# Moving layer 2's products into the tail of layer 1, and layer 3's weight in front of its aggregation

## The chip, the cores and the metric

The kernel runs on one core of one Trainium2 chip. The metric is the device time of one execution in microseconds; the times given are medians over runs. All times inside an execution are counted from the start of its profiled span.

## The reference

Four graph layers on x (4096 x 256, float32) with one dense adjacency matrix `adj` (4096 x 4096, zeros and ones, with self loops). Every layer ends with x = layernorm(x + layer(x)).

```python
# layer 0: relu([x, (adj @ x) / max(deg, 1)] @ W + b)
# layer 1: two steps n = 0, 1 of
#   A  = top-p softmax attention of Xa (rows cut to mass 0.9, renormalised)
#   Xf = R @ Xf          (R: row-normalised adj + I)
#   Xa = A @ Xa
#   Z += Xf @ U1[n].T + Xa @ U2[n].T        then layernorm(X + Z) * g + b
# layer 2: [x, adj @ x, e] @ weight + bias  (e: one number per node)
# layer 3: relu((A_norm @ x) @ W + b),  A_norm = (adj + I) scaled by d^-1/2 on both sides
```

Layers 2 and 3 are linear before their bias, and in both the weight can be applied before the aggregation as well as after it: (adj @ x) @ W = adj @ (x @ W). The change rests on this.

## The kernel before

Rows are cut into 32 tiles of 128 (NT = 32, P = 128, D = 256). A product with the adjacency takes, for each output tile, 32 matmuls 128x512: the right side holds the upper and the lower half of each number side by side (`split`, L140: 2 x 256 columns in the type fp32r), the left side is the adjacency, brought from memory in four pieces of 512 KB per tile by POOL's DMA queue into four buffers (`adj_piece`, L135; `adj_matmul`, L162). The two 256-column halves of the result are added afterwards.

Layer 1 works through its tiles with attention. Rows whose cut cannot be settled in the common way are put off: they are listed, and gathered into put-off tiles (`put_off`, L836; four of them in step 1). A put-off tile is a generator with stages: rows and logits; then `peak` and the exponentials; five probes in `bracket` (L440), each a pass of VectorE over 4096 columns (L464); candidates, `tops`, `pick`, and `flag` (L548). The flag of a put-off tile is a matmul with a column of ones (L554) into the bank `mm_bank`, a copy by ScalarE (L556), and a read of the value by VectorE, which in `settle` (L607) branches on it at L614; `settle` then writes the kept weights over the tile `e`. `finish` (L903) draws the remaining stages of a put-off tile and then makes its sums in `pieces` (L691): transposes of `e` (L712) and matmuls with xa (L737). What follows a tile's sums is returned by `after` (L806): s1 is `mix` (L784: transposes, four matmuls with U1 and U2 at L790), s2 the two layernorms and the store of x2 (`put`, L755, an indirect store on POOL's queue for put-off tiles). These are passed on in a list `last` and placed among the next tile's `pieces`.

At the end of step 1 two put-off tiles are left in `jobs` (L988); the list `last` of the third is worked off within the sums of the fourth.

Then come layers 2 and 3 in one block (L1026). Layer 2 loads x2 as halves (`load_halves`, L147, eight loads of 512 KB through two scratch buffers). For each tile `main` (L1038) makes the 32 matmuls, and `l2_end` (L1043) adds the halves, loads the tile's own x2, transposes both (four transposes), multiplies with the 512 rows of the weight (four matmuls at L1052), adds bias and the edge term, normalises, stores x3, scales it by d^-1/2 and splits it into the halves `yh` that layer 3 aggregates. In layer 3 `l3_end` (L1065) adds halves, its own term (x3 scaled by `dinv2`), transposes (two), multiplies with w3 (two matmuls at L1075), adds bias, relu, the residual, and normalises. `main` of a tile stands ahead of the end of the tile before it:

```python
for halves, end in ((lambda jt: x2h[:, jt, :], l2_end), ...):
    for it in range(NT):
        new = main(it, halves)
        if acc is not None:
            end(it - 1, acc)
```

Each engine has its own queue of instructions, in an order fixed when the program is built; an engine whose next instruction waits holds up all that stand behind it. `mm_bank` is one PSUM bank of 512 float32 columns, used as two halves of 256 in turn (`half`, L78).

Of the kernel before, what the change touches and what calls it, by code (L numbers as in the profile page):

```python
# [21 lines left out]
P = 128  # L22
D = 256
# [25 lines left out]
def gnn_stack(ctx, tc, x, adjt, adjn, w0, b0, w1, w2t, w3t, u1t, u2t, ln_g, ln_b, w2, b2, w3, b3, out):  # L49
# [55 lines left out]
    x1b_d = dram.tile([N, D], F32, name="x1b_d")  # L105
    x2_d = dram.tile([N + P, D], F32, name="x2_d")
    x3_d = dram.tile([N, D], F32, name="x3_d")
    xa_d = dram.tile([N + P, D], F32, name="xa_d")
    xf_d = dram.tile([N, D], F32, name="xf_d")
    list_d = [dram.tile([N + P, 1], I32, name=f"list{n}_d") for n in range(STEPS)]  # L110
# [36 lines left out]
    def load_halves(scratch, src, queue):  # L147


        xh = hpool.tile([P, NT, 2 * D], F32R, tag="H", name="xh")  # L150
        W = J0 * D
        for c in range(NT // J0):
            s = slice(c * J0, (c + 1) * J0)
            t, up = (scratch[:, k * W : (k + 1) * W].rearrange("p (j d) -> p j d", d=D) for k in (c % 2, 2 + c % 2))
            if queue is None:
                t = src[:, s, :]
            else:
                queue.dma_start(t, all_rows(src)[:, s, :])
            split(up.bitcast(I32), xh[:, s, :], t)
        return xh  # L160

# [33 lines left out]
    def ln_apply(dst, t, stats):  # L195
        mv, r = stats
        nc.vector.tensor_scalar(dst, t, mv[:, 0:1], r, op0=ALU.subtract, op1=ALU.mult)
# [17 lines left out]
    with tc.tile_pool(name="l0", bufs=1) as l0, tc.tile_pool(name="l0w", bufs=2) as l0w:  # L215
# [68 lines left out]
        def l0_end(it, agg):  # L284
            xi = l0w.tile([P, D], F32, tag="x0i", name="x0i")
            nc.scalar.dma_start(xi, rows(x, it))
            xt = transposed(xi, agg)
            ps = half("mm")
            for c in range(4):
                nc.tensor.matmul(ps, xt[:, c, :], w0_sb[:, c, :], start=(c == 0), stop=(c == 3))  # L290
            t = l0w.tile([P, D], F32, tag="t", name="t")
            nc.vector.tensor_add(t, ps, b0_sb)
            nc.vector.scalar_tensor_tensor(t, t, 0.0, xi, op0=ALU.max, op1=ALU.add)
            ln_apply(x1[:, it, :], t, ln_stats(t))

# [3 lines left out]
            nc.sync.dma_start(rows(x1b_d, it), x1b)  # L299

        def l0_keys(it):
            make_keys(transposed(x1[:, it, :]), kS[:, it * P : (it + 1) * P])
# [18 lines left out]
    with tc.tile_pool(name="l1", bufs=1, reuse_waits="tile") as l1:  # L321
# [484 lines left out]
        def after(n, st):  # L806


            def s1():
                st["h"] = mix(n, st)  # L810

            def s2():
                h = st["h"]
                mv, r = ln_stats(h)
                nc.vector.scalar_tensor_tensor(h, h, mv[:, 0:1], cur["g"], op0=ALU.subtract, op1=ALU.mult)
                nc.vector.scalar_tensor_tensor(h, h, r, st["x1"], op0=ALU.mult, op1=ALU.add)
                ln_apply(h, h, ln_stats(h))
                put(x2_d, st, h)

            return [s1] if n + 1 < STEPS else [s1, s2]  # L820

        def take_rows(n, slots, e):

# [59 lines left out]
        def run_step(n, es):  # L883
# [16 lines left out]
                    job["st"] = st  # L900
                return False

            def finish(job, last):  # L903
                while not advance(job):
                    pass
                ops = {}
                for k, fs in enumerate(last):
                    ops[k + 1] = fs
                cur["late"] = True
                pieces(n, job["st"], None, ops)  # L910
                cur["late"] = False
                return [[f] for f in after(n, job["st"])]
# [64 lines left out]
            if n == 0:  # L977
# [46 lines left out]


    with tc.tile_pool(name="l23", bufs=1, reuse_waits="tile") as l23:  # L1026
        w2_sb = load_w(l23, w2[: 2 * D, :], "w2_sb")
# [4 lines left out]
        x2h = load_halves(l23.tile([P, 4 * J0 * D], F32, name="scratch"), x2_d[:N, :], nc.sync)  # L1032

        yh = [pool.tile([P, NT // 2, 2 * D], F32R, tag="X", name=f"yh{k}") for k, pool in enumerate((xpool, l23))]
        dinv2 = l23.tile([P, NT], F32, name="dinv2")
        nc.vector.tensor_mul(dinv2, dinv, dinv)

        def main(it, halves):  # L1038
            acc = ps_acc.tile([P, 512], F32, tag=("acc", "nef")[it % 2], name="acc")
            adj_matmul(l23, acc, it, halves, JP)  # L1040
            return acc

        def l2_end(it, acc):  # L1043
            nn = l23.tile([P, D], F32, tag="agg", name="agg", bufs=2)
            nc.scalar.copy(nn, acc[:, :D])
            nc.vector.tensor_add(nn, nn, acc[:, D:])
            xi = l23.tile([P, D], F32, tag="res", name="x2i", bufs=2)
            nc.sync.dma_start(xi, rows(x2_d, it))
# [6 lines left out]
            nc.vector.scalar_tensor_tensor(t, w2e_sb, nef[:, it : it + 1], ps, op0=ALU.mult, op1=ALU.add)  # L1055
            nc.vector.tensor_add(t, t, xi)
            x3 = l23.tile([P, D], F32, tag="h", name="x3", bufs=2)
            ln_apply(x3, t, ln_stats(t))
            nc.sync.dma_start(rows(x3_d, it), x3)
            y = l23.tile([P, 1, D], F32, tag="y", name="y", bufs=2)  # L1060
            nc.vector.tensor_scalar(y[:, 0, :], x3, dinv[:, it : it + 1], None, op0=ALU.mult)
            up = l23.tile([P, 1, D], I32, tag="up", name="up", bufs=2)
            split(up, yh[2 * it // NT][:, it % (NT // 2), None, :], y)

        def l3_end(it, acc):  # L1065
            x3 = l23.tile([P, D], F32, tag="res", name="x3i", bufs=2)
            nc.sync.dma_start(x3, rows(x3_d, it))
            a = l23.tile([P, D], F32, tag="agg", name="agg", bufs=2)
            nc.scalar.activation(a, acc[:, :D], AF.Copy, scale=dinv[:, it : it + 1])
# [6 lines left out]
            t = l23.tile([P, D], F32, tag="t", name="t", bufs=2)  # L1076
            nc.vector.tensor_add(t, ps, b3_sb)
            nc.vector.scalar_tensor_tensor(t, t, 0.0, x3, op0=ALU.max, op1=ALU.add)
            o = l23.tile([P, D], F32, tag="h", name="o", bufs=2)
            ln_apply(o, t, ln_stats(t))  # L1080
            nc.sync.dma_start(rows(out, it), o)

        for halves, end in ((lambda jt: x2h[:, jt, :], l2_end), (lambda jt: yh[2 * jt // NT][:, jt % (NT // 2), :], l3_end)):
            acc = None
            for it in range(NT):
                new = main(it, halves)
                if acc is not None:
                    end(it - 1, acc)
                acc = new
            end(NT - 1, acc)  # L1090


# [39 lines left out]
```

## Time and profile before

| | us |
|---|---|
| time, median of 3 | 3500.99 (3497.21 to 3509.62) |
| span of the profiled execution | 3453.8 |
| TensorE matmul busy | 3070.8 (89%) |
| VectorE busy | 2372.2 (69%) |
| ScalarE busy | 1596.2 (46%) |
| GpSimd busy | 962.0 (28%) |
| L168, matmuls of layer 0 and 2 (2048) | 547.7 |
| L168, matmuls of layer 3 (1024) | 257.5 |

The profile is of one execution, shorter than the timed ones; differences are read within it. Layer 0 fills the first 460 us or so, layer 1 ends at about 2826 us with its last store of x2, layer 2's matmuls run to about 3151 and layer 3's to 3438. Matmuls are recorded as pipelined, each with its end, so that their durations overlap, and an f32 matmul shows as two records, an fp32r matmul as one. DMA share is the mean busy share of the 16 DMA engines.

### The profile page before, as it was taken

To read this page: it belongs to the slowest core of one execution; us is meant where nothing else is said; L and a number is where in the kernel's file an instruction comes from. 1 tells how busy PE (TensorE), PEld (TensorE's weight loads), DVE (VectorE), ACT (ScalarE), POOL (GpSimd) and SP (SyncE) were. 2 spreads that over 40 slices of the span, in tenths; PEclk is the share of its full clock that TensorE was granted. 3 is DMA by queue.
4 is the path that set the end of the run, shared out by engine and by line. 5 is a ranking of instruction groups with operands and counts; after the bars stand their busy time and mean duration, and the time that the engine had idled before them with its cause. 6 is when DMAs were issued, how large, how long until landed. Compare 5 with 4: busy or idle time off the path is not lost. (4 is left out here: it accounts for less than half of the span.)

```text
span 3453.8 us, 46253 instructions
## 1 busy us (share of the span) xinstructions
PE 3070.8 (89%) x14780; PEld 2501.1 (72%) x14780; DVE 2372.2 (69%) x7082; ACT 1596.2 (46%) x2846; POOL 962.0 (28%) x1234
## 2 busy tenths in 40 slices
PE   6888878999999999779998898999998549999998
PEld 4666657788888887557787777877787437887776
DVE  5666676788778887447888897889799654443333
ACT  3443356677777776436555454555554211111000
POOL 1222224666666666200000001000100112222332
PEclk8999989999999999789999999999999769999999
DMA  6777756777777776431000211011010038888886
GB/s 215 228 224 213 218 127 105 133 138 138 137 133 134 138 147 133 115 111 42 24 24 22 34 33 35 26 36 35 28 38 22 15 98 246 244 245 245 266 266 214
DMA packets 252192, 433.86 MB, mean 126 GB/s; under 512 B 35136, under 2 KB 177280, under 8 KB 251936
## 3 DMA queue, kind: packets, MB, share of 16 engines
q0 software_dynamic: 92544, 289.11, 34.8%
q1 hardware_dynamic: 142416, 125.73, 13.0%
q10 hardware_dynamic: 16976, 15.95, 1.5%
q8 instruction: 119, 1.95, 0.3%
q14 instruction: 137, 1.12, 0.1%
HBM read 423.45 MB, written 57.54 MB: 139 GB/s over the span
## 5 line engine op out<-in xcount | busy, mean ns | idle before, releaser
L652 PE MATMUL acc_r<-xh,adjq 128*128 128x512 f32 x2048 | 615.4, 431 | 22.8 <-ACT adjq L649 17.6
L168 PE MATMUL acc<-xh,adjt 128*128 128x512 f32 x2048 | 547.7, 422 | 92.3 <-DMA adjt<-in_adjt 65.5
L737 PE MATMUL acc_bank<-xa,at 128*128 128x256 f32 x2304 | 563.3, 385 | 30.1 <-ACT at L715 29.6
L638 POOL DMA_INDIRECT G<-x_d,cols x512 | 502.0, 981 | 281.9 <-PE acc_bank L729 153.3
L168 PEld LDWEIGHTS acc<-xh,adjt 128*128 128x128 f32 x2048 | 400.3, 200 | 204.5 <-DMA adjt<-in_adjt 74.1
L737 PEld LDWEIGHTS acc_bank<-xa,at 128*128 128x128 f32 x2304 | 421.7, 192 | 90.7 <-ACT at L715 40.7
L652 PEld LDWEIGHTS acc_r<-xh,adjq 128*128 128x128 f32 x2048 | 380.7, 192 | 118.2 <-ACT adjq L649 42.9
L649 ACT CAST adjq<-adj 128x512 fp32r<-128x512 uint8 x512 | 316.0, 619 | 292.9 <-PE acc_r L652 94.5
L399 DVE MAX8 cand<-e 128x8 f32<-128x256 f32 x1024 | 381.5, 415 | 92.0 <-ACT e L381 91.0
L137 POOL DMA_DIRECT2D adjt<-in_adjt x384 | 209.4, 545 | 700.3 <-PE acc L168 346.9
L380 PE MATMUL lg<-kS,q 128*128 128x512 f32 x1104 | 393.4, 442 | 9.8 <-ACT e L381 9.6
L381 ACT COPY e<-lg 128x512 f32<-128x512 f32 x552 | 319.5, 585 | 177.6 <-PE lg L380 176.5
L192 POOL TENSOR_TENSOR rstd<-ve,mhalf 128x1 f32<-128x1 f32 x168 | 107.7, 641 | 843.8 <-DVE ve L190 797.5
L729 PE MATMUL acc_bank<-G,dg 128*128 128x256 f32 x1024 | 274.7, 389 | 39.8 <-DMA G<-x_d,cols 24.9
L496 DVE FIND_INDEX8 cols<-top,e 128x8 uint32<-128x4096 f32 x64 | 282.8, 4419 | 0.0
L168 PE MATMUL acc<-yh,adjt 128*128 128x512 f32 x1024 | 257.5, 403 | 4.7 <-DMA adjt<-in_adjt 4.4
L729 PEld LDWEIGHTS acc_bank<-G,dg 128*128 128x128 f32 x1024 | 194.3, 193 | 87.5 <-DMA G<-x_d,cols 36.1
L715 ACT COPY at<-at_ps 128x512 f32<-128x512 f32 x296 | 173.7, 589 | 145.3 <-PE at_ps L712 143.9
L168 PEld LDWEIGHTS acc<-yh,adjt 128*128 128x128 f32 x1024 | 190.0, 188 | 50.3 <-PE tr L178 4.5
L712 PE MATMUL at_ps<-ident,e 128*128 128x128 f32 x1184 | 183.8, 279 | 39.8 <-DVE e L629 26.9
L712 PEld LDWEIGHTS at_ps<-ident,e 128*128 128x128 f32 x1184 | 152.0, 145 | 75.6 <-issue 34.2
L380 PEld LDWEIGHTS lg<-kS,q 128*128 128x128 f32 x1104 | 183.5, 193 | 31.8 <-ACT e L381 18.5
(274 smaller groups left out, 4583.3 us busy)
## 6 DMA issues: line engine op xcount, KB each, us to landing
adjt<-in_adjt POOLq DMA_DIRECT2D x384, 512.0 KB
adj<-adj_d SPq DMA_DIRECT2D x256, 128.0 KB
adj_d<-a SPq DMA_DIRECT2D x128, 128.0 KB
adjn<-in_adjn POOLq DMA_DIRECT2D x64, 256.0 KB
x_d<-x SPq DMA_DIRECT2D x64, 128.0 KB
G<-x_d,cols POOLq DMA_INDIRECT x512
xf_d<-xf_new SPq DMA_DIRECT2D x64, 128.0 KB
xf<-xf_d SPq DMA_DIRECT2D x64, 128.0 KB
```

The costliest lines, as they stand in the source:

```text
L137: nc.gpsimd.dma_start(t, src[it, :, c * jp : (c + 1) * jp, :])
L168: nc.tensor.matmul(acc, a[:, j, :], halves(jt), start=(jt == 0), stop=(jt == NT - 1))
L380: nc.tensor.matmul(pl[:, :LC], q[k], kS[:, s], start=(k == 0), stop=(k == 1))
L381: nc.scalar.copy(l[:, s], pl[:, :LC])
L399: nc.vector.max(dst[:, 8 * g : 8 * g + 8], src[:, g * GW : (g + 1) * GW])
L496: nc.vector.max_index(st["at"][:, 8 * r : 8 * r + 8], t8, st["e"][:, :N])
L638: nc.gpsimd.indirect_dma_start(out=g, out_offset=None, in_=x1_d, in_offset=bass.IndirectOffsetOnAxis(ap=st["at"][:, k : k + 1], axis=0))
L649: nc.scalar.copy(a, cur["a8"][:, g % 2 * GP : (g % 2 + 1) * GP, :])
L652: nc.tensor.matmul(acc_r, a[:, j, :], xf[:, jt, :], start=(jt == 0), stop=False)
L712: nc.tensor.transpose(ps[:, j, :], e[:, (g * G + j) * P : (g * G + j + 1) * P], ident)
L729: nc.tensor.matmul(acc_a, dg[:, k % 4, :], st["G"][k], start=(k == 0), stop=(k == KEPT - 1))
L737: nc.tensor.matmul(acc_a, ats[g][:, j, :], cur["xa"][:, jt, :], start=(jt == 0), stop=(jt == NT - 1))
```

## The change

Three parts belong together.

1. x2 is multiplied with layer 2's weight already in layer 1. A new tensor zu in memory holds for each row 512 numbers: z = x2 @ (rows of the weight that belong to the neighbours), and u = x2 @ (rows that belong to the node itself). Before the last put-off tile of step 1 is finished, `last` is worked off, the weight is loaded into a tile `e` that is free by then (`z_room`), and after each stage of the put-off tile that `finish` draws, three of the 32 tiles of zu are made (`zu_tile`): load the tile of x2, two transposes, two f32 matmuls of 128x512, a copy by ScalarE, a store. Since `zu` needs 512 columns it writes the whole of `mm_bank`. The rows of the last put-off tile get their zu after their x2 is known.
2. Layer 2 aggregates the halves of z, so that after the aggregation no product is left: `l2_end` adds the halves, the edge term, u, x2 and the bias. It loads one more tile (u) than before.
3. Layer 3's weight is applied to layer 2's result, before the aggregation (`l2_y`, two tiles later in the order): two transposes and two matmuls, then ScalarE scales by d^-1/2 and the result is split. `l3_end` has no product left; it takes its own term from `yh`.

Part 1's order in TensorE's queue, as the changed program has it: the flag's matmul of the last put-off tile stands behind the transposes of 30 zu tiles and the matmuls of 27.

The diff, cut to its core:

```diff
+        def z_room(e):
+            w = e[:, : 4 * D].rearrange("p (c o) -> p c o", c=2)
+            for k in range(2):
+                nc.sync.dma_start(w[:, :, k * D : (k + 1) * D],
+                                  w2[(1 - k) * D : (2 - k) * D, :].rearrange("(c p) o -> p c o", p=P))
+            cur["z"] = {"w": w, "x": e[:, 4 * D : 8 * D].rearrange("p (k o) -> p k o", o=D),
+                        "out": e[:, 8 * D : 16 * D].rearrange("p (k o) -> p k o", o=2 * D), "n": 0}
+        def zu(x):
+            z = cur["z"]
+            xt = transposed(x)
+            ps = mm_bank.rearrange("p h o -> p (h o)")
+            for c in range(2):
+                nc.tensor.matmul(ps, xt[:, c, :], z["w"][:, c, :], start=(c == 0), stop=(c == 1))
+            out = z["out"][:, z["n"] % 4, :]
+            z["n"] += 1
+            nc.scalar.copy(out, ps)
+            return out
+        def zu_tile(i):
+            x = cur["z"]["x"][:, i % 4, :]
+            nc.sync.dma_start(x, rows(x2_d, i))
+            nc.sync.dma_start(rows(zu_d, i), zu(x))
...
-            def finish(job, last):
+            def finish(job, last, todo=()):
                 while not advance(job):
-                    pass
+                    for i in todo[:3]:
+                        zu_tile(i)
+                    todo = todo[3:]
+                for i in todo:
+                    zu_tile(i)
...
-            for job in jobs:
-                last = finish(job, last)
+            for k, job in enumerate(jobs):
+                todo = []
+                if n > 0 and k + 1 == len(jobs):
+                    for fs in last:
+                        for f in fs:
+                            f()
+                    last = []
+                    z_room(es[1 - NT % 2])
+                    todo = list(range(NT))
+                last = finish(job, last, todo)
...
         def l2_end(it, acc):
...
-            xt = transposed(xi, nn)
-            ps = half("mm")
-            for c in range(4):
-                nc.tensor.matmul(ps, xt[:, c, :], w2_sb[:, c, :], start=(c == 0), stop=(c == 3))
+            u = l23.tile([P, D], F32, tag="u", name="u", bufs=2)
+            nc.sync.dma_start(u, rows(zu_d, it)[:, D:])
             nc.vector.tensor_add(xi, xi, b2_sb)
+            nc.vector.tensor_add(u, u, xi)
...
+        def l2_y(it, x3):
+            xt = transposed(x3)
+            ps = half("mm")
+            for c in range(2):
+                nc.tensor.matmul(ps, xt[:, c, :], w3_sb[:, c, :], start=(c == 0), stop=(c == 1))
             y = l23.tile([P, 1, D], F32, tag="y", name="y", bufs=2)
-            nc.vector.tensor_scalar(y[:, 0, :], x3, dinv[:, it : it + 1], None, op0=ALU.mult)
+            nc.scalar.activation(y[:, 0, :], ps, AF.Copy, scale=dinv[:, it : it + 1])
...
         def l3_end(it, acc):
...
-            nc.vector.scalar_tensor_tensor(a, acc[:, D:], dinv[:, it : it + 1], a, op0=ALU.mult, op1=ALU.add)
-            nc.vector.scalar_tensor_tensor(a, x3, dinv2[:, it : it + 1], a, op0=ALU.mult, op1=ALU.add)
-            xt = transposed(a)
-            ps = half("mm")
-            for c in range(2):
-                nc.tensor.matmul(ps, xt[:, c, :], w3_sb[:, c, :], start=(c == 0), stop=(c == 1))
+            own = y_halves(it).bitcast(F32)
+            for part in (own[:, :D], own[:, D:], acc[:, D:]):
+                nc.vector.scalar_tensor_tensor(a, part, d, a, op0=ALU.mult, op1=ALU.add)
```

More of the change, by code (lines that the diff above doesn't have):

```diff
@@ L107, in gnn_stack @@
     x3_d = dram.tile([N, D], F32, name="x3_d")
+    zu_d = dram.tile([N + P, 2 * D], F32, name="zu_d")
     xa_d = dram.tile([N + P, D], F32, name="xa_d")
@@ L145, in split, with load_halves @@
         nc.vector.tensor_sub(dst[:, :, D:], src, up.bitcast(F32))
-    def load_halves(scratch, src, queue):
+    def load_halves(scratch, src, queue, cols=slice(None)):
         xh = hpool.tile([P, NT, 2 * D], F32R, tag="H", name="xh")
@@ L157, in load_halves @@
             else:
-                queue.dma_start(t, all_rows(src)[:, s, :])
+                queue.dma_start(t, all_rows(src)[:, s, cols])
             split(up.bitcast(I32), xh[:, s, :], t)
@@ L299, in l0_end @@
             nc.sync.dma_start(rows(x1b_d, it), x1b)
+            if it == NT - 1:
+                nc.sync.dma_start(rows(x2_d, it), x1[:, it, :])
         def l0_keys(it):
@@ L818, in s2 @@
                 put(x2_d, st, h)
+                if "z" in cur:
+                    put(zu_d, st, zu(h))
             return [s1] if n + 1 < STEPS else [s1, s2]
+        def z_room(e):
[19 more added lines that the diff above has]
+            nc.sync.dma_start(rows(zu_d, i), zu(x))
         def take_rows(n, slots, e):
@@ L1026, in gnn_stack @@
     with tc.tile_pool(name="l23", bufs=1, reuse_waits="tile") as l23:
-        w2_sb = load_w(l23, w2[: 2 * D, :], "w2_sb")
+        zh = load_halves(l23.tile([P, 4 * J0 * D], F32, name="scratch"), zu_d[:N, :], nc.sync, slice(0, D))
         w2e_sb = load_bcast(l23, w2[2 * D, :], "w2e_sb")
@@ L1031, in gnn_stack, with y_halves @@
         b3_sb = load_bcast(l23, b3, "b3_sb")
-        x2h = load_halves(l23.tile([P, 4 * J0 * D], F32, name="scratch"), x2_d[:N, :], nc.sync)
         yh = [pool.tile([P, NT // 2, 2 * D], F32R, tag="X", name=f"yh{k}") for k, pool in enumerate((xpool, l23))]
-        dinv2 = l23.tile([P, NT], F32, name="dinv2")
-        nc.vector.tensor_mul(dinv2, dinv, dinv)
+        def y_halves(jt):
+            return yh[2 * jt // NT][:, jt % (NT // 2), :]
         def main(it, halves):
@@ L1048, in l2_end @@
             nc.sync.dma_start(xi, rows(x2_d, it))
-            xt = transposed(xi, nn)
-            ps = half("mm")
-            for c in range(4):
-                nc.tensor.matmul(ps, xt[:, c, :], w2_sb[:, c, :], start=(c == 0), stop=(c == 3))
+            u = l23.tile([P, D], F32, tag="u", name="u", bufs=2)
+            nc.sync.dma_start(u, rows(zu_d, it)[:, D:])
             nc.vector.tensor_add(xi, xi, b2_sb)
+            nc.vector.tensor_add(u, u, xi)
             t = l23.tile([P, D], F32, tag="t", name="t", bufs=2)
-            nc.vector.scalar_tensor_tensor(t, w2e_sb, nef[:, it : it + 1], ps, op0=ALU.mult, op1=ALU.add)
-            nc.vector.tensor_add(t, t, xi)
-            x3 = l23.tile([P, D], F32, tag="h", name="x3", bufs=2)
+            nc.vector.scalar_tensor_tensor(t, w2e_sb, nef[:, it : it + 1], nn, op0=ALU.mult, op1=ALU.add)
+            nc.vector.tensor_add(t, t, u)
+            x3 = l23.tile([P, D], F32, tag="h", name="x3", bufs=3)
             ln_apply(x3, t, ln_stats(t))
             nc.sync.dma_start(rows(x3_d, it), x3)
+            return x3
+        def l2_y(it, x3):
[3 more added lines that the diff above has]
+                nc.tensor.matmul(ps, xt[:, c, :], w3_sb[:, c, :], start=(c == 0), stop=(c == 1))
             y = l23.tile([P, 1, D], F32, tag="y", name="y", bufs=2)
-            nc.vector.tensor_scalar(y[:, 0, :], x3, dinv[:, it : it + 1], None, op0=ALU.mult)
+            nc.scalar.activation(y[:, 0, :], ps, AF.Copy, scale=dinv[:, it : it + 1])
             up = l23.tile([P, 1, D], I32, tag="up", name="up", bufs=2)
-            split(up, yh[2 * it // NT][:, it % (NT // 2), None, :], y)
+            split(up, y_halves(it)[:, None, :], y)
         def l3_end(it, acc):
@@ L1068, in l3_end @@
             a = l23.tile([P, D], F32, tag="agg", name="agg", bufs=2)
-            nc.scalar.activation(a, acc[:, :D], AF.Copy, scale=dinv[:, it : it + 1])
-            nc.vector.scalar_tensor_tensor(a, acc[:, D:], dinv[:, it : it + 1], a, op0=ALU.mult, op1=ALU.add)
-            nc.vector.scalar_tensor_tensor(a, x3, dinv2[:, it : it + 1], a, op0=ALU.mult, op1=ALU.add)
-            xt = transposed(a)
-            ps = half("mm")
-            for c in range(2):
-                nc.tensor.matmul(ps, xt[:, c, :], w3_sb[:, c, :], start=(c == 0), stop=(c == 1))
@@ L1076, in l3_end @@
[L1076 to L1080, printed above, removed]
-            nc.sync.dma_start(rows(out, it), o)
[L1083 to L1090, printed above, removed]
+            d = dinv[:, it : it + 1]
@@ new lines, in l3_end @@
+            nc.scalar.activation(a, acc[:, :D], AF.Copy, scale=d)
+            own = y_halves(it).bitcast(F32)
+            for part in (own[:, :D], own[:, D:], acc[:, D:]):
+                nc.vector.scalar_tensor_tensor(a, part, d, a, op0=ALU.mult, op1=ALU.add)
+            nc.vector.tensor_add(a, a, b3_sb)
+            nc.vector.scalar_tensor_tensor(a, a, 0.0, x3, op0=ALU.max, op1=ALU.add)
+            o = l23.tile([P, D], F32, tag="h", name="o", bufs=3)
+            ln_apply(o, a, ln_stats(a))
@@ new lines, in l3_end @@
+            nc.sync.dma_start(rows(out, it), o)
+        done = []
+        for it in range(NT):
+            acc = main(it, lambda jt: zh[:, jt, :])
+            if it > 1:
+                l2_y(it - 2, done.pop(0))
+            if it > 0:
+                done.append(l2_end(it - 1, last))
+            last = acc
+        l2_y(NT - 2, done.pop(0))
+        l2_y(NT - 1, l2_end(NT - 1, last))
+        for it in range(NT):
+            acc = main(it, y_halves)
+            if it > 0:
+                l3_end(it - 1, last)
+            last = acc
@@ L1093 @@
+        l3_end(NT - 1, last)
 def kernel(x, adj, L0_gnn_W, L0_gnn_b, L1_gnn_W1, L1_gnn_W2, L1_gnn_W3, L1_gnn_U1, L1_gnn_U2,
```

## The prediction

> **What bounds the kernel now.** I read the page first (busy shares, the 40 slices), then busy time by windows for the end of the program, then the time order of single instructions there, because the change touches nothing before about 2700 us: in the order in which the instructions stand on each engine, the changed program is the same up to there, but for one row-store in layer 0.
>
> ```profile
> PE   6888878999999999779998898999998549999998
> PEclk8999989999999999789999999999999769999999
> DMA  6777756777777776431000211011010038888886
> ```
>
> The reader is to see two things on the right: a dip of TensorE (slices "5 4") at the end of layer 1's second step, and after it two layers in which TensorE is full and the DMA engines are busy for eight tenths. The same in windows (columns: window, length, PE, PEld, DVE, ACT, POOL with their counts, granted clock, DMA share, GB/s):
>
> ```profile
> 2734.00:2772.00 38.00, 0.14 (x2) 0.09 (x2) 36.13 (x103) 0.05 (x1) 1.02 (x1) 0.53 0.01 3
> 2772.00:2791.00 19.00, 0.31 (x4) 0.29 (x3) 15.90 (x12) 0.15 (x1) 0.00 (x0) 0.50 0.00 1
> 2791.00:2826.00 35.00, 23.86 (x120) 20.00 (x118) 10.21 (x30) 6.24 (x11) 9.68 (x13) 0.84 0.38 112
> 2826.00:2861.00 35.00, 22.68 (x71) 16.67 (x72) 16.27 (x19) 8.94 (x10) 3.71 (x7) 0.68 0.71 211
> 2861.00:3151.00 290.00, 290.00 (x1317) 235.07 (x1317) 117.98 (x328) 40.66 (x91) 82.02 (x150) 1.00 0.81 245
> 3151.00:3438.00 287.00, 282.19 (x1230) 222.84 (x1228) 97.99 (x263) 25.04 (x67) 86.12 (x157) 1.00 0.85 261
> ```
>
> For 57 us (2734 to 2791) VectorE works alone on the last put-off tile. Then that tile's sums and layer 2's start (to 2861), then layer 2 with TensorE always busy (290 us for 30 tiles, 9.67 each), and layer 3 nearly so. The change fills the 57 us with TensorE work and takes TensorE work out of the two layers. Everything hangs on two questions: does the new work end within the gap, and can the layers run faster than TensorE lets them now?
>
> The gap, in order of time:
>
> ```profile
> 2733.89 0.41 DVE L197 TENSOR_SCALAR h<-h,bn,rstd 128x256 f32<-128x256 f32 x1 [0.45 <-POOL rstd L192]
> ...
> 2771.64 0.16 DVE L530 SCALAR_TENSOR_TENSOR bad_l<-left_l,bad_l 128x1 f32<-128x1 f32 x1
> 2771.86 0.19 PE L554 MATMUL mm_bank<-ones_col,bad_l 128*1 128x1 f32 x2 [38.32 <-DVE bad_l L530]
> 2772.08 0.15 ACT L556 CAST nbad_l<-mm_bank 1x1 int32<-1x1 f32 x1 [38.04 <-PE mm_bank L554]
> 2773.34 0.24 DVE L620 TENSOR_SCALAR go_l<-upto,left_l 128x24 f32<-128x24 f32 x1 [1.54 <-DVEq L614]
> ```
>
> VectorE needs TensorE once in the middle: the flag `bad` is summed by a tiny matmul (L554), copied by ScalarE (L556) and read back (L614) before `settle` goes on.
>
> **What the Trainium skill says.** PSUM — Partial Sum Buffer, "The four PSUM rules": one matmul output fills at most one bank, 512 fp32 columns. `zu` makes outputs of just that size in the one bank `mm_bank`, so a tile's matmuls cannot start before the former tile's copy has left the bank; the flag's matmul uses the same bank. No run shows that yet. TensorE: Matmul & The Clock Gate, "Part 1: The HAM clock gate": after an idle window of about 3.4 us the array runs at half rate. The trace agrees: clock 0.50 in the gap, and the first eight transposes after it take 1.94 us against 1.04 elsewhere. SBUF — State Buffer, "Who interferes with whom": GpSimd and some VectorE operations lock each other out. Here `rstd` on POOL took 4.58 us beside a VectorE scan (L464) and 0.59 without one. DMA: Bandwidth & Descriptors, "Specifications", gives some 358 GB/s of HBM for a core. The trace does not come near it: 261 GB/s at a share of 0.85 and 245 at 0.81 both stand for 302 to 307 GB/s at a full share, and the measurement decides.
>
> **The change part by part.**
>
> *The zu loop in the gap.* It may begin only when the third put-off tile's x2 is stored, since it reads x2 back from memory. That tile's `mix` and norms, till now done within the last tile's sums, come first. TensorE ends its sums at 2733.5; VectorE takes `h` up after the third probe (ends 2740.4), the extra operations push the next probe by 1.9 us (the same operations for another tile, 2725.2 to 2728.9, took 3.75 against 1.82 without), the second `rstd` waits for that probe, so `h` is done at about 2749.5, the store lands some 4 us after it (4.6 us lie between the last put at 2821.00 and the first load at 2825.58, under load), the load of a tile takes about 2 us (estimate), transposes and their copy 1: the first matmul at about 2757.
>
> One tile: two f32 matmuls 128x512. The trace has f32 passes of 128 and 256 columns only, two passes a matmul: 4 passes of 128 in 0.71 us, 8 of 256 in 1.99, 0.2 of each being the end of the last. The cost goes with the columns, so 512 take 0.43 a pass: 4 passes 1.72 and 0.2 for the end. Lower bound: 0.24 a pass as fp32r passes of 512 take, upper 0.86 at half rate. I take 0.43. Then ScalarE's copy of 128x512 (0.59, as L715) and two handovers (0.02 and 0.05). That is 2.6 us, in series because of the one bank; transposes (0.22) and their copies lie within. Loads and stores (384 KB a tile) are four tiles ahead. 32 tiles are 83 us where 57 were free.
>
> In the changed order of TensorE's queue, L554 stands behind the matmuls of 27 zu tiles (and 30 tiles' transposes), and L556 behind the 27th copy on ScalarE. So the flag comes at 2757 + 27 x 2.6 + 2.5 (first window at half rate) = 2830 instead of 2771.9: +58 us. Behind it VectorE's whole `settle` waits (17 us), and behind that the transposes and sums of the last tile; the other five zu tiles (13 us) are hidden beside `settle`. The `bad` flag itself is late by 3 us only, hidden.
>
> *Behind the flag.* The sums lose the other tile's `mix` (4 transposes 0.44, matmuls 1.80): -2.2. After the last x2 a zu product follows: transposes 0.45 and matmuls 3.6 at half rate (TensorE idle for 5 us before), copies 0.37 and 0.59, the start of the put: about +5. The first four adjacency pieces, issued at 2807 to 2822 before the load of x2's halves, now stand behind the put of zu in POOL's queue, so 2 MB move beside that load: 0 to 7 us, I take +3.5. The gap and the start cost 58 - 2.2 + 5 + 3.5 = +64.
>
> *Layer 2.* Per tile 4 transposes and 4 matmuls become 2 and 2: 2 x 0.11 + 4 passes x 0.213 = 1.07 less, 9.67 becomes 8.60 for TensorE. Its DMA: four adjacency pieces (2.10 MB), x2, x3 and new `u` (0.13 each) are 2.49 MB; at 8.60 that is 290 GB/s. *Layer 3.* All transposes and matmuls go: 8.71 becomes 7.64; with 2.36 MB that is 309 GB/s. Even now layer 3 shows TensorE held up by pieces at a lower rate:
>
> ```profile
> 3220.00:3230.00 10.00, 10.00 (x45) 7.92 (x45) 3.41 (x11) 0.74 (x2) 3.83 (x7) 1.00 0.76 235
> 3230.00:3240.00 10.00, 9.32 (x41) 7.13 (x40) 3.34 (x9) 0.74 (x2) 2.76 (x5) 1.00 0.93 283
> ...
> 3330.00:3340.00 10.00, 9.18 (x42) 7.33 (x41) 3.00 (x8) 0.74 (x2) 2.74 (x6) 1.00 0.86 263
> ```
>
> Where TensorE (first number after the length) falls short, DMA is at 263 to 283 GB/s. So the DMA queue becomes the bound in both layers. Bounds for its rate: 270 (what such windows show now) and 304 (a full share). I take 285: layer 2 8.74 a tile, -28 over 30 tiles; layer 3 32 x 8.28 + 1 = 266 instead of 287, -21. VectorE's two added operations in layer 3 (0.48 each) and ScalarE's `y` are hidden: VectorE is busy for 98 of 287 us.
>
> *The end.* The last tile loses a transpose, copy, matmul chain and gains two VectorE operations: -2. Sum: 64 - 28 - 21 - 2 = +13.
>
> **The rivals.** *Level:* DMA gives 295 to 300: layer 2 at TensorE's 8.60, -32, layer 3 at 7.95, -32: sum -2, 3499 us. For it: single windows of 10 us in layer 3 reach a share of 0.93 and 283 GB/s. *Faster:* TensorE stays the bound, 8.60 and 7.64: -32 and -40, and 64 - 74 = -10, 3491; with a zu pass at the lower bound of 0.24 another -20. Against it: it needs 309 GB/s, above what a full share gives. *Half-rate zu loop:* gaps of 0.6 us in each 2.6 us count as idle; 27 x 1.8 = 48 more, 3562. Against it: layer 0's windows with TensorE busy for 17 of 20 us keep 0.91 to 1.00. *Poor DMA:* 270 and less: layer 2 9.2, layer 3 8.75, +14 to +22 on the forecast, 3530 to 3540. *The gap holds it all:* if the flag passed early, +64 would be +8, and 3458 the time; the fixed order in TensorE's queue speaks against it.
>
> **How the numbers follow.** Forecast (slower by some 13 us) 0.46; level 0.28; faster 0.10, of which early flag 0.02; poor DMA 0.09; half rate 0.07. The likeliest gives 3501 + 13 = 3514 us. Part of the forecast's case lies within 10.5 us of now, so: faster 0.12, same 0.36, slower 0.52. The range of 3488 to 3545 takes in level, most of faster and poor DMA, and leaves the half-rate loop out.
>
> **What would show it.** Right: L554 at about 2830 behind the 27th zu product, VectorE idle for some 50 us before it, zu tiles at 2.6 us, layer 2's first full tiles some 60 us later, DMA shares above 0.9 with TensorE waiting for adjacency pieces in layer 3, tiles of 8.7 and 8.3 us. Wrong: L554 before 2800; zu tiles under 2 or over 4 us; layer 3 at 7.7 us with TensorE full.

## The result, and the profile after

| | before | after |
|---|---|---|
| time, median | 3503.91 us (3497.21 to 3509.62, 4 runs) | 3597.89 us (3595.46 to 3600.73, 4 runs) |
| ratio | | 1.0271, 95% interval 1.0252 to 1.0289 |
| span of the profiled execution | 3453.8 us | 3595.3 us |

The change makes the kernel slower by 94 us. The forecast was 3514, with a range that ended at 3545.

The profiled execution of before is shorter than its timed ones, by some 50 us that go missing before the change begins (in stages that both programs share), so I set the two traces against each other from a common mark on: the maximum over the last put-off tile (L437 before, L442 after), at 2712.2 and 2766.6 us. Times "in before's clock" below have these 54.4 us taken off.

The three lines of the page that answer to those of before:

```profile
PE   6888878999999997789988899999997658888997
PEclk8999998999999999889999999999998879999999
DMA  7767755777777676241001110111110337777997
```

The dip of TensorE is "7 6 5" instead of "5 4": the gap is filled, but not gone. Layer 2 follows with "8 8 8 8" where before had "9 9 9 9", and the DMA engines stand at seven tenths there, which is less than before although each tile moves more. Only in layer 3, the last slices, do they come near the share that was forecast. The same in windows (columns: window, length, then busy time of PE, PEld, DVE, ACT and POOL with counts, granted clock, DMA share, GB/s):

```profile
2789.00:2827.00 38.00, 18.31 (x50) 8.85 (x50) 35.88 (x99) 5.63 (x13) 10.14 (x7) 0.73 0.29 93
2827.00:2884.00 57.00, 46.85 (x132) 20.35 (x130) 1.77 (x12) 19.07 (x45) 0.00 (x0) 1.00 0.42 143
2884.00:2904.00 20.00, 10.89 (x27) 4.46 (x27) 16.26 (x12) 3.75 (x8) 0.00 (x0) 0.89 0.21 79
2904.00:2982.00 78.00, 50.28 (x193) 36.85 (x191) 27.62 (x53) 15.82 (x22) 11.29 (x19) 0.77 0.49 156
2982.00:3310.00 328.00, 270.60 (x1121) 214.09 (x1121) 109.03 (x321) 44.20 (x116) 83.08 (x147) 0.95 0.73 225
3310.00:3581.00 271.00, 250.19 (x1043) 190.21 (x1041) 112.43 (x292) 18.55 (x41) 85.72 (x157) 1.00 0.89 276
```

In the second row VectorE is busy for 1.77 of 57 us: it waits for the flag (the matmul L559 in this kernel), as forecast. The fifth row is the surprise. In layer 2 nothing is full: TensorE 270.6 of 328 us, DMA 0.73, VectorE a third. Where no resource is full, something waits in turn, and the question is for what.

To see where the 94 us come from I cut both traces at ScalarE's first and last copy of a sum in layer 2 and in layer 3 (L1045 and L1069 before; L1092 and L1123 after):

| stage (us) | before | after | difference |
|---|---|---|---|
| tail: from the mark to layer 2's first copy | 147.4 | 210.3 | +62.9 |
| layer 2, 31 tiles | 291.4 (9.40 a tile) | 333.2 (10.75) | +41.8 |
| to layer 3's first copy | 12.1 | 11.8 | -0.3 |
| layer 3, 31 tiles | 274.8 (8.86) | 259.3 (8.36) | -15.5 |
| end | 15.9 | 14.1 | -1.8 |
| sum | 741.6 | 828.7 | +87.1 |

The tail went as forecast (+64), layer 3 nearly (-21), the end too (-2). Layer 2 was to fall by 28 and rose by 42.

**Layer 2's loop.** The engines' waits between 2982 and 3310 us in the kernel after (us in total, times, longest):

```profile
POOL rstd L194 <- DVE ve L192: 189.2, 28, 8.7
DVE x2i L1098 <- DMA x2i<-x_d: 176.7, 28, 7.6
...
PE acc L170 <- DMA adjt<-in_adjt: 57.0, 29, 4.6
```

VectorE stands for 6.3 us a tile at L1098, the addition of the bias to the tile's own x2, and what it waits for is that load. GpSimd waits for VectorE in front of `rstd`, and behind `rstd` in its queue stand the next issues of adjacency pieces, for which TensorE then waits. The chain of waits gives one round of it (start, length, what):

```profile
3082.60 0.42 DVE x2i L1098
3083.02 0.34 DVE agg L1093
3083.39 0.50 DVE t L1101
3083.91 0.44 DVE t L1102
3084.37 0.44 DVE bn L188
3084.83 0.18 DVE bn L190
3085.40 0.68 POOL rstd L194
3086.11 0.42 DVE x L199
3086.55 0.32 SPq L1105
3086.96 6.35 DMA x2i<-x_d
3093.41 0.43 DVE x2i L1098
```

The row that VectorE adds to at 3093.41 was requested at 3086.96, only when VectorE was through with the former round. The same round in time order (here and in the time orders below, other instructions between the lines shown are left out):

```profile
3086.03 1.15 POOL L139 DMA_DIRECT2D adjt<-in_adjt  x2
3086.46 0.43 DVE L1099 TENSOR_TENSOR u<-u,x2i 128x256 f32<-128x256 f32 x1
3086.96 0.38 SPq L1095 DMA_DIRECT2D x2i<-x_d  x1
...
3093.41 0.43 DVE L1098 TENSOR_TENSOR x2i<-x2i,b_sb 128x256 f32<-128x256 f32 x1 [6.52 <-DMA x2i<-x_d]
3093.75 0.41 DVE L1093 TENSOR_TENSOR agg<-agg,acc 128x256 f32<-128x256 f32 x1
```

Counted from the layer's start, this is the addition for the 15th row, its load is the 15th, and the `agg` behind it is that of the 12th tile. In VectorE's fixed order the addition L1098 of a later tile stands right behind the last use of its buffer (`u += x2i`, L1099, here of the 13th row; there are two buffers) and ahead of the next `agg`. So the buffer becomes free, the load is issued, and VectorE's very next instruction waits for that load: 6.35 us of load and some 4 us of work in series, round by round.

Before had such an addition ahead of `agg` too, but no loop. Its time order around one load:

```profile
2999.72 0.43 DVE L1056 TENSOR_TENSOR t<-t,x2i 128x256 f32<-128x256 f32 x1
3000.21 0.32 SPq L1048 DMA_DIRECT2D x2i<-x_d  x1
3001.75 0.41 DVE L197 TENSOR_SCALAR x<-t,bn,rstd 128x256 f32<-128x256 f32 x1 [0.74 <-POOL rstd L192]
3002.19 0.32 SPq L1059 DMA_DIRECT2D x_d<-x  x1
...
3005.95 0.43 DVE L1053 TENSOR_TENSOR x2i<-x2i,b_sb 128x256 f32<-128x256 f32 x1 [2.56 <-PE tr L178]
...
3015.63 0.42 DVE L1053 TENSOR_TENSOR x2i<-x2i,b_sb 128x256 f32<-128x256 f32 x1 [2.56 <-PE tr L178]
```

There the last use of x2i is `t += x2i`, ahead of the LayerNorm. By count the load at 3000.21 is the 17th; the addition at 3005.95 is still that of the 16th row, and the 17th row's stands at 3015.63. So 15.4 us lie between the load and the addition that needs it, and the addition waits not for the load but for TensorE's transposes (2.56 us), which stand behind main matmuls in TensorE's order.

### The profile page after: what moved, and what is told of

The parts are those of the page before. It is cut to its first block, busy times and chain, and to the rows that moved or that the text cites. A ratio compares the mean times of both kernels' runs of the same rounds, so it can differ in the third digit from the quotient of the medians.

```text
span 3595.3 us, 46174 instructions
## 1 busy us (share of the span) xinstructions
PE 3115.8 (87%) x14594; PEld 2485.8 (69%) x14594; DVE 2381.1 (66%) x7113; ACT 1619.9 (45%) x2912; POOL 962.1 (27%) x1235
## 3 DMA queue, kind: packets, MB, share of 16 engines
q1 hardware_dynamic: 156928, 143.17, 14.1%
## 5 line engine op out<-in xcount | busy, mean ns | idle before, releaser
L742 PE MATMUL acc_bank<-xa,at 128*128 128x256 f32 x2304 | 571.1, 389 | 33.9 <-ACT at L720 33.4
L170 PE MATMUL acc<-yh,adjt 128*128 128x512 f32 x1024 | 247.9, 396 | 20.4 <-DMA adjt<-in_adjt 17.9
L182 ACT COPY xt<-tr 128x256 f32<-128x256 f32 (+1 forms) x267 | 120.0, 450 | 198.2 <-PE tr L180 179.8
L717 PE MATMUL at_ps<-ident,e 128*128 128x128 f32 x1184 | 184.7, 280 | 28.1 <-DVE e L634 14.9
```

What stands on the lines that cost most here:

```text
L170: nc.tensor.matmul(acc, a[:, j, :], halves(jt), start=(jt == 0), stop=(jt == NT - 1))
L717: nc.tensor.transpose(ps[:, j, :], e[:, (g * G + j) * P : (g * G + j + 1) * P], ident)
L742: nc.tensor.matmul(acc_a, ats[g][:, j, :], cur["xa"][:, jt, :], start=(jt == 0), stop=(jt == NT - 1))
```

## The experiments

My theory after the traces was this loop. Its rivals were: the DMA carries too much (u's 128 KB a tile); the loaded rows have too few buffers; the order in SyncE's queue, where the load stands behind the x3 store, holds it. For all runs the same cuts as above (us; a tile in layers 2 and 3):

| run | median, ratio to before (95%) | tail | layer 2 | layer 3 |
|---|---|---|---|---|
| before | 3503.91 | 147.4 | 9.40 | 8.86 |
| after | 3597.89, 1.0271 (1.0252 to 1.0289) | 210.3 | 10.75 | 8.36 |
| e1_bufs | 3587.59, 1.0243 (1.0222 to 1.0264) | 212.0 | 10.35 | 8.41 |
| e2_no_u | 3527.22, 1.0083 (1.0060 to 1.0107) | 207.8 | 8.69 | 8.42 |
| e5_late_adds | 3532.42, 1.0081 (1.0062 to 1.0101) | 209.8 | 8.57 | 8.42 |
| e10_store_queue | 3594.49, 1.0249 (1.0220 to 1.0279) | 209.7 | 10.41 | 8.29 |
| e11_u_late | 3530.79, 1.0068 (1.0046 to 1.0089) | 209.5 | 8.51 | 8.43 |
| e12_tail_alone | 3564.80, 1.0164 (1.0130 to 1.0199) | 208.2 | 9.44 | 8.81 |
| e3_two_banks | 3574.35, 1.0205 (1.0188 to 1.0223) | 191.1 | 10.73 | 8.44 |
| e6_late_banks | 3508.89, 1.0011 (0.9997 to 1.0026) | 191.5 | 8.64 | 8.42 |
| e7_early_zu | 3501.59, 0.9988 (0.9976 to 1.0000) | 181.0 | 8.55 | 8.39 |
| e8_rest_after | 3494.59, 0.9970 (0.9958 to 0.9983) | 174.7 | 8.59 | 8.46 |
| e9_fold_x2 | 3492.64, 0.9961 (0.9946 to 0.9975) | 176.3 | 8.51 | 8.38 |

The ratio is taken against runs of before on the same chip, whose medians were 3501.76 (e1 to e5), 3505.39 (e6 to e9) and 3505.29 (e10 to e12).

**More buffers (e1).**

```diff
-            xi = l23.tile([P, D], F32, tag="res", name="x2i", bufs=2)
+            xi = l23.tile([P, D], F32, tag="res", name="x2i", bufs=4)
...
-            u = l23.tile([P, D], F32, tag="u", name="u", bufs=2)
+            u = l23.tile([P, D], F32, tag="u", name="u", bufs=4)
...
-            x3 = l23.tile([P, D], F32, tag="res", name="x3i", bufs=2)
+            x3 = l23.tile([P, D], F32, tag="res", name="x3i", bufs=4)
```

> Four buffers in place of two for the loaded x2i and x3i rows and for u. Loop theory (VectorE's fixed order puts the add of b2 to a row that is still to be loaded ahead of the next tile's agg, and the load can start only when the buffer is freed just before): with four buffers the same add only moves to tile k+8, right behind the add that frees its buffer, so layer 2 stays at 10.5 to 11 us a tile and the total within 10 us of the changed kernel, 3590 to 3600. Rival, too few buffers: layer 2 falls to about 8.7 us a tile, 66 us less, 3532.

10.35 us a tile, total 3587.6, 10 us less than after. Twice the buffers leave the loop where it was:

```profile
3074.28 0.43 DVE L1099 TENSOR_TENSOR u<-u,x2i 128x256 f32<-128x256 f32 x1
3074.73 0.35 SPq L1095 DMA_DIRECT2D x2i<-x_d  x1
3081.63 0.43 DVE L1098 TENSOR_TENSOR x2i<-x2i,b_sb 128x256 f32<-128x256 f32 x1 [6.93 <-DMA x2i<-x_d]
```

The program's order moved with the buffers. The addition is now that of the 18th row, ahead of the 11th tile's `agg`, and it again stands right behind the release of its buffer (by the 14th row). In both traces VectorE's additions run as far ahead as there are buffers, so that each waits for a load just issued.

**Without u (e2).** This kernel leaves u out of layer 2's sum; it serves for its times alone.

```diff
-            u = l23.tile([P, D], F32, tag="u", name="u", bufs=2)
-            nc.sync.dma_start(u, rows(zu_d, it)[:, D:])
             nc.vector.tensor_add(xi, xi, b2_sb)
-            nc.vector.tensor_add(u, u, xi)
...
-            nc.vector.tensor_add(t, t, u)
+            nc.vector.tensor_add(t, t, xi)
```

> Layer 2 without u: its load and the add of it are left out of the result, so 128 KB less are moved for a tile. Loop theory: the wait for x2i stays in the loop, only one transfer fewer stands beside it: 10 to 10.8 us a tile, total 3570 to 3592. Rival, the added bytes bind (2.49 MB a tile in place of 2.36): layer 2 falls by 5 per cent of its tile at the same rate at the least, and to the 8.3 us that the DMA needs for 2.36 MB at 285 GB/s if the rate recovers: 3515 to 3580 and a DMA share of over 0.9 there.

8.69 us a tile, total 3527.2: my expectation for the loop was missed. The rival's range holds the time, but its DMA share of over 0.9 did not come (0.85 with 265 GB/s in layer 2, from 2970 to 3237 us). The run changes two things: it takes bytes away, and with `t += xi` it also puts the last use of x2i ahead of LayerNorm again, as in before. It can't tell them apart. The next two runs do.

**All additions behind the sum (e5).**

```diff
-            nc.vector.tensor_add(xi, xi, b2_sb)
-            nc.vector.tensor_add(u, u, xi)
...
-            nc.vector.tensor_add(t, t, u)
+            for part in (b2_sb, u, xi):
+                nc.vector.tensor_add(t, t, part)
```

> In layer 2, b2, u and x2 are each added to t after agg, instead of to the loaded rows ahead of it, so that no instruction that waits for a load stands in front of the next tile's agg in VectorE's order; the same bytes, buffers and products. Loop theory: layer 2 at 8.7 us a tile with a DMA share above 0.85, total 3530 to 3540. Rivals: if the DMA's rate is the limit, or GpSimd's queue with the adjacency issues behind the LayerNorm power, the tile stays at 10.5 to 11 and the total at 3590 to 3600.

3532.4, and 8.57 us a tile. Layer 2 of this run in a window:

```profile
2995.00:3258.00 263.00, 256.21 (x1130) 204.71 (x1130) 111.68 (x332) 44.38 (x117) 82.22 (x150) 1.00 0.92 285
```

With the same bytes, buffers, engines and number of additions, the DMA share goes from 0.73 to 0.92 and the rate from 225 to 285 GB/s. Neither u's bytes nor GpSimd's queue (its `rstd` still stands ahead of the adjacency issues) was the limit. TensorE is busy for 256.2 of the 263 us.

**Only u and x2i late (e11).**

```diff
             nc.vector.tensor_add(xi, xi, b2_sb)
-            nc.vector.tensor_add(u, u, xi)
...
-            nc.vector.tensor_add(t, t, u)
+            for part in (u, xi):
+                nc.vector.tensor_add(t, t, part)
```

> The changed kernel with b2 still added early to the loaded x2i, but u and x2i each added to t after agg; all bytes, buffers and loads as in the changed kernel. The buffer of x2i is then freed ahead of LayerNorm instead of behind it, so that the load has some 3 us more before VectorE stands at the early add. Loop theory: 8.6 to 9 us a tile, total 3530 to 3540, which would say that the gain of the run without u came from this order and not from its bytes. Rival, u's bytes or the early add as such are the cause: 10 to 10.9 a tile, 3580 to 3598.

8.51 us a tile and 3530.8, with the early addition of b2 still there. Time order around one load in this run:

```profile
3094.40 0.42 DVE L1102 TENSOR_TENSOR t<-t,x2i 128x256 f32<-128x256 f32 x1
3095.14 0.32 SPq L1095 DMA_DIRECT2D x2i<-x_d  x1
3099.34 0.42 DVE L1098 TENSOR_TENSOR x2i<-x2i,b_sb 128x256 f32<-128x256 f32 x1 [3.33 <-DMA x2i<-x_d]
3099.68 0.41 DVE L199 TENSOR_SCALAR x<-t,bn,rstd 128x256 f32<-128x256 f32 x1
3100.11 0.32 SPq L1105 DMA_DIRECT2D x_d<-x  x1
```

VectorE still stands for 3.33 us at the addition, but the load was issued behind `t += x2i` and before the LayerNorm result, which VectorE makes only after the addition. The wait ends before `agg` is due (3101.85). So it is not the early addition as such, and not u's bytes; it is the release of the buffer directly ahead of the instruction that needs it again. From a load's issue to its addition it is 4.5 us here (median of 32), against 6.7 in the changed kernel, where in the round shown two adjacency pieces are issued within a microsecond ahead of the load; what shortened the load itself no run separates.

**The store in another queue (e10).**

```diff
-            nc.sync.dma_start(rows(x3_d, it), x3)
+            nc.scalar.dma_start(rows(x3_d, it), x3)
```

> The changed kernel with the x3 store of layer 2 issued by ScalarE instead of SyncE, so that the load of the next x2i no longer stands behind the store in SyncE's order; VectorE's order stays. Loop theory: the load is still held by its buffer, which VectorE frees only after the LayerNorm result, so it is issued at most 0.5 us sooner: 10.3 to 10.8 us a tile, total 3583 to 3598. Rival, the store in SyncE's order is what holds the load: 8.7 us a tile, 3533.

10.41 us a tile, 3594.5: no gain that can be measured. One round in time order:

```profile
3102.46 0.41 DVE L199 TENSOR_SCALAR x<-t,bn,rstd 128x256 f32<-128x256 f32 x1 [0.45 <-POOL rstd L194]
3102.87 0.42 DVE L1099 TENSOR_TENSOR u<-u,x2i 128x256 f32<-128x256 f32 x1
3102.90 0.33 ACTq L1105 DMA_DIRECT2D x_d<-x  x1
3103.32 0.32 SPq L1095 DMA_DIRECT2D x2i<-x_d  x1
3107.92 0.42 DVE L1098 TENSOR_TENSOR x2i<-x2i,b_sb 128x256 f32<-128x256 f32 x1 [4.63 <-DMA x2i<-x_d]
```

The load is free of the store and still starts only as L1099 ends (3102.87 + 0.42 = 3103.29; the issue at 3103.32). SyncE's order was not what held it.

**The tail alone (e12).** This is the changed kernel up to the end of layer 1, and the code of before from layer 2 on, so that the products are made and stored but not used; the diff is the whole of the change's first part.

> The kernel before with the products of x2 in step 1's tail and their stores, but layers 2 and 3 as before, so that the products are not used. If the tail's price is a term of its own, as the traces say (57.7 us until the settling flag, 68 instead of 47 after it would include the late start of layer 2, which belongs to the tail: 58 + 68 = 126), the total is 3504 + 120 to 126 = 3624 to 3630. If a part of the 68 belongs to layer 2's new code instead, 3570 to 3615.

3564.8, +59.5 (46 to 70 by the interval), and +60.8 in the trace (208.2 against 147.4). My expectation was a wrong sum: it put the whole 68 us of a stretch behind the flag on top of the 58, although by its own words 47 of them stood in before already, and that stretch was read at a later cut than the table's. The total is below both ranges that I had named. By the table's cuts (+63) the run agrees: the tail's price is a term of its own, and layers 2 and 3 stay at 9.44 and 8.81.

**Two banks for the products (e3).**

```diff
-            ps = mm_bank.rearrange("p h o -> p (h o)")
+            ps = ps_lg.tile([P, 512], F32, tag="lg", name="z_ps")
```

> The products of x2 in two PSUM banks in turn instead of in one. If the single bank makes each tile in the tail wait for its copy (2.66 us a tile: 4 matmuls 1.98, copy 0.59), a tile takes about 2.0 us, the matmul of the settling flag comes 27 x 0.65 = 18 us sooner, and the total falls by 18, to 3580. Rival, another wait sets the tail's rate (the load of the x2 row, the store): no change, 3598.

3574.4, 23.5 less than after; the tail falls by 19.2 us in the trace. In time order, TensorE alone:

```profile
2838.77 0.19 PE L559 MATMUL mm_bank<-ones_col,bad_l 128*1 128x1 f32 x2
2839.36 3.70 PE L844 MATMUL z_ps<-e,xt 128*128 128x512 f32 x8 [0.39 <-ACT xt L182]
...
2890.51 3.70 PE L844 MATMUL z_ps<-e,xt 128*128 128x512 f32 x8 [0.51 <-ACT xt L182]
2894.04 1.04 PE L717 MATMUL at_ps<-ident,e 128*128 128x128 f32 x8
```

The size is right, the way to it was not. A tile takes 2.33 us (two in 4.65), because the transposes of two tiles now stand between the products, and the products wait for ScalarE's copy of them (0.51 a pair). And the flag comes after 8 products instead of 27, at 2838.8 - 62.4 (this run's mark against before's) = 2776.4 in before's clock, 5 us later than before instead of 57. Yet the sums of the last put-off tile (L717) start at 2894.04, behind all products, although VectorE's last pass of `settle` (L634) had ended at 2863.00. With the flag early, what the tail costs is the length of the 32 products in TensorE's queue, which the sums stand behind; the late flag is only one way in which that length shows.

**Towards a version that beats both (e6 to e9).** e6 is e5 and e3 together.

> The late adds of e5 and the two banks of e3 together. If the two causes are separate terms of the sum (the loop in layer 2, 65 us; the single bank in the tail, 18 to 23 us), they add: 3532 - 20 = 3512. If they share a cause, less than 10 us are gained on e5.

3508.9: the two terms add, and the kernel is level with before. e7 begins the products without working off the third put-off tile first:

```diff
-                    for fs in last:
-                        for f in fs:
-                            f()
-                    last = []
                     z_room(es[1 - NT % 2])
```

> As e6, and the products of x2 begin without finishing the third put-off tile first, so that the first load of x2 rows no longer waits for that tile's store. TensorE stood 17 us in the changed kernel between the last product of the third put-off tile and the first of x2. Theory (the tail is bound by TensorE's queue of 32 product tiles, from their start on): 14 to 17 us less than e6, 3497. Rival (the settling of the last tile on VectorE is what ends last): no gain, 3512.

3501.6, 7 less, where I expected 14 to 17; the tail falls by 10.5 us in the trace. The products start 15 us sooner (2797.1 - 56.6 = 2740.5 in before's clock, against 2755.5 in e6), but the third tile's `mix` goes back among the last tile's sums (2.2 us, the amount that the forecast had taken off for it), and one more product is made there for that tile (2.3); that these two are the missing 4.5 us is worked out, not shown by a run. e8 keeps 8 of the 32 tiles until after the last tile's `mix`:

```diff
+                todo, rest = todo[:-8], todo[-8:]
                 while not advance(job):
...
+                if "z" in cur:
+                    for i in cur["z"].pop("rest", ()):
+                        zu_tile(i)
```

> As e7, with 8 of the 32 product tiles left until after the put-off tile's sums, in the room where TensorE waits for LayerNorm and the store. Theory (the sums stand behind products in TensorE's order although the settling is done): the sums start as soon as the settling is done, and of the 8 x 2.33 = 19 us some 8 go into the wait: 5 to 10 us less than e7, 3490. Rival: the stores and the load of the P halves wait for the 8 late tiles, and as much is lost behind the sums as is won ahead of them: 3497, or more.

3494.6, 7 less, as expected.

e9 adds x2 to u on GpSimd in the tail, so that layer 2 loads one row tile less.

```diff
             nc.scalar.copy(out, ps)
+            nc.gpsimd.tensor_add(out[:, D:], out[:, D:], x)
...
-            xi = l23.tile([P, D], F32, tag="res", name="x2i", bufs=2)
-            nc.sync.dma_start(xi, rows(x2_d, it))
...
-            for part in (b2_sb, u, xi):
+            for part in (b2_sb, u):
```

> As e8, with x2 added to its own product U on GpSimd in the tail before it is stored, so that layer 2 loads 128 KB less a tile (2.36 MB in place of 2.49). If the DMA's rate bounds layer 2 now (8.57 us a tile in e5), the tile falls to 2.36/2.49 of it, 8.15, but no lower than what TensorE needs, about 8.3: 31 x 0.27 = 8 us less than e8, 3482. If TensorE or something else bounds it, no gain; if GpSimd's adds delay the tail, slower than e8.

3492.6, where 3482 was expected if the DMA's rate set layer 2: not to be told from e8. Its layer 2:

```profile
2950.00:3212.00 262.00, 256.65 (x1133) 205.84 (x1133) 101.27 (x305) 44.71 (x117) 82.98 (x151) 1.00 0.89 271
```

The bytes are fewer (271 GB/s for the same tiles in the same time) and the tile is hardly faster (8.51 against 8.59 in e8, where the DMA's rate would have given 8.15), so the DMA's rate does not set layer 2 at 8.5 us: TensorE is busy for 98% of the window. e9 is 0.39% faster than before (0.25 to 0.54), e8 0.30% (0.17 to 0.42): the idea of the change pays a little, once the loop and more than half of the tail's price are gone (174.7 - 147.4 = 27 us are left of it in e8).

## Why the prediction was wrong

*The start and rate of the products: right.* Forecast 2757 and 2.6 us a tile, measured 2755.6 (in before's clock) and 2.66:

```profile
2817.09 1.98 PE L844 MATMUL mm_bank<-e,xt 128*128 128x512 f32 x4 [0.46 <-ACT e L847]
2819.75 1.98 PE L844 MATMUL mm_bank<-e,xt 128*128 128x512 f32 x4 [0.46 <-ACT e L847]
...
2883.59 0.19 PE L559 MATMUL mm_bank<-ones_col,bad_l 128*1 128x1 f32 x2 [0.46 <-ACT e L847]
...
2903.38 1.94 PE L717 MATMUL at_ps<-ident,e 128*128 128x128 f32 x8 [6.74 <-DVE e L634]
```

Each tile waits 0.46 us for the copy to leave the one bank. The Trainium skill's PSUM — Partial Sum Buffer, "The four PSUM rules", says only that an output fills at most one bank; that the next product must wait followed from the program, which has one bank for all of them. With two banks (e3) a tile is 0.33 us shorter. The half-rate rival fell: the clock is 1.00 in the second window, with these waits in it.

*The flag: right.* Forecast 2830, measured 2883.59 - 54.4 = 2829.2. *The sum of the tail: right*, +64 against +62.9, and +59.5 for the tail alone. The way was as forecast: the flag is late, `settle` behind it, and the sums wait for `settle` (the last line above, 6.74 us behind the products). The forecast was too narrow, though, in making the flag the only way: in e3 the flag is early, and 44 us of the 63 stay, since the sums stand behind the same products.

*Layer 3: right in size, 5 us off, its bound not shown.* TensorE, now busy for 238.8 of 259 us from 3322 to 3581, waits for adjacency pieces, as forecast (17.7 us at the matmuls and 24.4 at the weight loads), at a DMA share of 0.89 and 279 GB/s. But GpSimd, which issues the pieces, also waits longer for VectorE ahead of `rstd` (33.0 us there, 3.1 in before's layer 3). Whether the DMA's rate or the time of the issues sets the 8.36 us no run separates. The forecast used 285 GB/s; 8.36 us a tile came out instead of 8.28, and before's own tile is 8.86 by this cut rather than 8.97.

*Layer 2: this is the step that failed.* "So the DMA queue becomes the bound in both layers. ... I take 285: layer 2 8.74 a tile, -28 over 30 tiles." The tile took 10.75 us, and the term was +42 instead of -28: 70 of the 84 us by which the forecast of 3514 was missed. I asked only which resource would be full, TensorE or the DMA, and took every load of layer 2 as hidden. No step priced the load of x2i against the place of its first use in VectorE's order, though the order of the changed program could be read: the release of the buffer had moved from ahead of LayerNorm to behind it, directly ahead of the addition that waits for the new load. e5 and e11 show that the size would have been right without the loop: with the release moved back, layer 2 takes 8.57 and 8.51 us at 285 and 286 GB/s, and the total, 3532 and 3531, is within the forecast's range. The bound was not right even then. In e5 TensorE is busy for 97% of layer 2, and e9 with fewer bytes is hardly faster, so it is TensorE that comes nearer to being the bound there. The forecast's two figures, 8.74 by the DMA and 8.60 by TensorE, lie so close together that the size would have come out with the wrong bound, by luck. The range left the loop out because none of the rivals was a wait of VectorE. Two sums among the rivals are also off, with nothing hanging on them: at 270 GB/s the forecast's own tiles give 14 + 15 = 29 us more, not 14 to 22, and without the 58 us of the flag the tail would be +6, not +8.

What stays open: without the loop (e5) the trace stands 21 us above before (762.3 against 741.6) where 13 were forecast; most of the rest is layer 3 (-14 in e5, -21 forecast). The timed median stands 31 above (22 to 35 by the interval). That difference of 10 us between the trace and the times I can't place.

## What to carry to other kernels

Where no engine and no queue is full over a stage, look for a loop of waits; follow one round of it in the chain of waits, from the load back to the instruction that freed its buffer. When a change moves the last reader of a loaded tile, ask where in the engine's fixed order the first use of the next load into that buffer stands. Here twice the buffers changed little, since the first use moved ahead with them; moving the last reader, or putting the additions with a loaded operand behind the sum that they belong to, took the loop away. Count loads and uses from the start of the stage when you pair them: the nearest use in time need not be that of the load you look at. Work put into a gap of one engine's queue still costs time where it is longer than the gap and later work stands behind it, even when the small instruction that seemed to be held up is moved ahead (e3).

## What the runs showed of the hardware

A load of 128 KB took 6.35 us from issue to landing in layer 2 of the changed kernel, beside the adjacency pieces of 512 KB, at a DMA share of 0.73 over the stage; another round shows 4.36. In the tail, waits of 0.46 us in every 2.66 us left TensorE's granted clock at 1.00 for 57 us. GpSimd's addition of 128x256 numbers in e9 mostly took 0.72 us; one beside a VectorE pass over 4096 columns took 3.88, and that pass 4.87 instead of 4.49.
